# Selective scan: the products with C taken for two directions at once, u for four rows at once, and part of the diagonals on GpSimd

## The chip, the cores and the metric

The kernel runs on one core of a Trainium2 chip. A core has five engines that work side by side, each through its own list of instructions in order: TensorE (PE, with a separate record PEld for its weight loads), VectorE (DVE), ScalarE (ACT), GpSimd (POOL) and SyncE (SP), which here only issues DMA transfers. They meet through semaphores. SBUF is the working memory, PSUM the memory that PE writes; both have 128 partitions. The metric is the device time of one execution in microseconds (us).

## The reference, cut to what matters

Four images of 56 x 56 places and 128 channels go through four layers, each added to its input after a group normalization: attention (L0), a selective scan (L1), a deformable convolution (L2), attention again (L3). All is float32. Of L1, the scan is:

```python
delta = softplus(delta + delta_bias)               # 256 inner channels d, 3136 places
def step(h, inp):                                  # h: [4 directions of an image, d, 16 states n]
    u_i, d_i, b_i, c_i = inp
    dA = jnp.exp(d_i[..., None] * A)
    h = h * dA + (d_i * u_i)[..., None] * b_i[:, None, :]
    y = jnp.einsum('gdn,gn->gd', h, c_i)
    return (h, y)
# xs: the places row by row, column by column, and both reversed;
# delta, B and C are the same for the four directions
```

The four directions' y are brought back to the order of places and added. Of L2, nine offsets for each place say where four neighbours are to be read; the reading positions are the offsets plus a fixed table of places (tap and place, no data in it).

## The kernel before, in words

`run` takes the images one after the other, and in each the layers one after the other. The scan is `mamba_scan` (line 875). Channels lie on partitions, in two halves j of 128. The image's 56 rows are taken two at a time (a step s, 28 of them); a group g = 2s + j is such a step for one half, 56 groups an image. A unit u is one row r (of two) in one direction d (of four) of a group: 8 units a group, 448 an image. A chunk is two steps, 224 places, the piece in which delta, B and C come from DRAM (`chunk`, tiles `xd` and `dl`).

For each group, `inputs_of` (L982) makes: `du`, delta times u, for each direction on POOL (`mult`, L994), 112 places each; `da`, the 16 decays exp(delta A) on ACT (L1002); and `du` split into parts (`high` on ACT, `low` on POOL, `low2` on ACT), turned on PE and kept as `ut`. For each step, `rows` (L936) makes from B the diagonals `dgb` (`b_diag`, L952): B, turned on PE into the PSUM tile `pb`, times a mask of ones on the diagonal, [112, 16 x 28], two for each row, on DVE, 16 to 6 units ahead of the step's first unit; and from C the tile `cb`, C spread over all partitions.

A unit is then: `inputs` (L1048) multiplies `ut` with `dgb` on PE, which spreads du times B over 16 states x 56 places into a PSUM bank `dbu` (two such); `inject` (L1059, ACT) puts the carried state in front; `scan` (L1066, DVE) is one instruction over 16 x 58 columns into one half of the SBUF tile `hs`, which holds a pair of directions (three such tiles); `save` (L1070, ACT) keeps the last state; `weigh` (L1075, POOL) multiplies the 16 x 56 states with `cb`, in place; `add_up` (L1084, PE) adds the 16 states by transposing them into one PSUM tile `yt`; `sum_out` (L1093, ACT) copies a pair's sums to `ys`; and for a group `back` (L1100, PE) and `back_add` (L1105, DVE) add them to the result `ya`.

The order is written out by hand: nothing reorders it. The loop at L1116 goes through the units, and each engine's list is what the loop emits for it, with two dictionaries of further work by unit: `soon` (the decays) and `plan` (all else, by `at(t, f)`). In step u of the loop stand save(u-1), inputs(u+1), the decays, weigh(u-1), scan(u), inject(u+1), add_up(u-3), sum_out, and then `plan`. The tiles `pbt`, `pcb`, `pt` and `pyb` share two PSUM banks (tag `mm`).

In `deform` (L1232) the normalized image is written to a table in DRAM by eight DMAs on SP (L1279, table `tab`, filled with zeros once at the start of the program), the offsets are convolved on PE, the positions are made of the offsets plus `base`, the table of places, on DVE (L1315 to L1324), and POOL then issues nine indirect DMAs for each 112 places (L1248). `base` is one of the columns of the constants' pack, which is loaded into SBUF at the start and stays there.

Of the kernel before, what the change touches and what calls it, by code (L numbers as in the profile page):

```python
# [19 lines left out]
P = 128  # L20
HW = 56
# [33 lines left out]
def _swin_cols():  # L55
# [6 lines left out]
    "C": [("ident", 128), ("gmat", 128), ("center1", 128), ("center2", 128), ("others2", 128), ("ones1", 1), ("ones2", 1), ("lo", 1), ("dmask", TB), ("halves", HW), ("base", 2 * KK * NTB)],  # L62
# [16 lines left out]
class _Net:  # L79
    def __init__(self, ctx, tc, x, packs, out):  # L80
# [5 lines left out]
        self.w = {}  # L86
        for i, (layer, cols) in enumerate(COLS.items()):
            at, n = _offsets(cols)
            t = wp.tile([P, n], F32, tag=f"w_{layer}", name=f"w_{layer}")
            (nc.sync if i % 2 == 0 else nc.scalar).dma_start(t, packs[layer])  # L90
            self.w[layer] = {name: t[:, o : o + k] for name, (o, k) in at.items()}
# [783 lines left out]
    def mamba_scan(self, b, xa, ya, s1):  # L875
# [10 lines left out]
        with tc.tile_pool(name="ms", bufs=2) as sb, tc.tile_pool(name="ms_ps", bufs=2, space=PSUM) as ps, tc.manual_schedule():  # L886
# [12 lines left out]
            def chunk(c):  # L899
# [31 lines left out]
                at(first - 22, high)  # L931
                at(first - 20, low)
                at(first - 18, low2)
                at(first - 14, both)

            def rows(s):  # L936
# [13 lines left out]
                def b_diag(r, tb):  # L950
                    t = m[r, tb] = sb.tile([TK, NST, TB], F32R, tag="dgb", name="dgb", bufs=8)
                    nc.vector.tensor_tensor(  # L952
                        t,
                        m["pb"][:TK, tb * NX + DTR : tb * NX + DTR + NST][:, :, None].to_broadcast([TK, NST, TB]),
                        dmask[:, None, :].to_broadcast([TK, NST, TB]),
                        ALU.mult,
                    )
# [15 lines left out]
                for r in range(2):  # L973
                    t = first - 16 + 8 * r
                    at(t, lambda r=r: b_rows(r))
                    for tb in range(2):
                        at(t + 1 + tb, lambda r=r, tb=tb: b_diag(r, tb))
# [4 lines left out]
            def inputs_of(g):  # L982

# [7 lines left out]
                def mult(d):  # L991
                    if d == 0:
                        m["du"] = sb.tile([P, 4, 2 * HW], F32, tag="du", name="du", bufs=1)
                    nc.gpsimd.tensor_tensor(m["du"][:, d, :].rearrange("p (r t) -> p r t", t=HW), dl(), self.direction(xa[:, j, :], d, 2 * s, 2), ALU.mult)  # L994
# [9 lines left out]
                def high():  # L1004
                    m["dh"] = sb.tile([P, 4, 4, 4, TB], F32R, tag="dh", name="dh", bufs=1)
                    du = m["du"].rearrange("p d (s t) -> p (d s) t", t=TB)
                    nc.scalar.copy(flat(m["dh"])[:, :, 0:2, :], du[:, :, None, :].to_broadcast([P, 16, 2, TB]))

                def low():
                    du = m["du"].rearrange("p d (s t) -> p (d s) t", t=TB)  # L1010
                    nc.gpsimd.tensor_tensor(flat(m["dh"])[:, :, 2, :], du, flat(m["dh"])[:, :, 0, :].bitcast(F32), ALU.subtract)
# [9 lines left out]
                def keep(i):  # L1021
                    m["ut", i] = sb.tile([TK, 4, P], F32R, tag="ut", name="ut", bufs=7)
                    nc.scalar.copy(m["ut", i].rearrange("k d c -> k (d c)"), m.pop(("pt", i))[:TK, :])

                for d in range(4):
                    at(first + d, lambda d=d: mult(d))
# [14 lines left out]
            def inputs(u):  # L1041
# [4 lines left out]
                for tb in range(2):  # L1046
                    for h in range(2):
# [3 lines left out]
                            rhs=made["r", g // 2][r, tb][:, 8 * h : 8 * h + 8, :].rearrange("k n t -> k (n t)"),  # L1051
# [9 lines left out]
            def scan(u):  # L1061
                g, r, d = units[u]
                if d % 2 == 0:
                    pairs[u // 2] = sb.tile([P, 2, NST, RW], F32, tag="hs", name="hs", bufs=3)
# [7 lines left out]
            def weigh(u):  # L1072
                g, r, d = units[u]
                hs = pairs[u // 2][:, d % 2, :, 2:]
                nc.gpsimd.tensor_tensor(hs, hs, made["r", g // 2]["cb"][:, :, r * HW : (r + 1) * HW], ALU.mult)  # L1075
# [15 lines left out]
            def sum_out(q):  # L1091
                backs[q] = sb.tile([YR, 2, P], F32, tag="ys", name="ys", bufs=6)
# [14 lines left out]
            for s in range(HW // 2):  # L1107
# [3 lines left out]
                for g in (2 * s, 2 * s + 1):  # L1111
                    inputs_of(g)
                    at(8 * g + 14, lambda g=g: back(g))
# [386 lines left out]
```

## Time and profile before

| what | value |
|---|---|
| median of 12 runs | 13417.06 us (13411.72 to 13436.87) |
| the profiled execution | 13425.0 us, its span 13423.2 us |
| busy over the span | PE 11694.9 us (87%), DVE 9588.2 (71%), ACT 7557.2 (56%), POOL 9942.3 (74%) |
| the scan of the first image, first scan to last | 995.19 to 2013.32 us |
| from the last scan to the first gather | 2013.32 to 2120.35 us |
| scans (L1066) | 1792, median 2068 ns |
| products with C (L1075) | 1792, median 1942 ns |

The profile is one execution. A group of instructions has a line of kernel.py, an engine, an operation, the tiles (out<-in) with shapes, a count, and then its busy time in us, the mean of one in ns, and the idle time of the engine just before them with what ended it. In the order of time a line has its start, its length, the instructions merged in it (x5) and, in brackets, the idle time before it. The 40 slices show the busy share of an engine in tenths; four images are four times ten slices. An instruction's record is somewhat longer than the distance to the start of the next one behind it, as they overlap a little.

### The profile page before, as it was taken

How to read it: one execution, taken by the hardware profiler on the slowest of the kernel's cores; microseconds unless marked ns; L12 is line 12 of the kernel's file. 1: busy time of each engine (PE TensorE's matmuls, PEld its weight loads, DVE VectorE, ACT ScalarE, POOL GpSimd, SP SyncE). 2: the span in 40 equal slices, each digit the busy share in tenths (PEclk: the TensorE clock that was granted, in tenths of full speed). 3: DMA queues.
4: the chain of work that ended last, by engine and by line, in shares of the span. 5: the costliest groups of instructions: out<-in, count | busy, mean ns of one | idle time of the engine just before them, and what ended most of it. 6: DMA issues, size and time to landing. Idle time of an engine off the chain costs nothing. (4 is left out here: it accounts for less than half of the span.)

```text
span 13423.2 us, 218271 instructions
## 1 busy us (share of the span) xinstructions
PE 11694.9 (87%) x85716; PEld 7453.1 (56%) x85716; DVE 9588.2 (71%) x11883; ACT 7557.2 (56%) x19130; POOL 9942.3 (74%) x6852
## 2 busy tenths in 40 slices
PE   8989994699998999469999899946999989994699
PEld 4448883444544888344454488834445448883444
DVE  6659995664664999656466599955646659995664
ACT  5567762356556776235655677623565567762356
POOL 4949994397594999439759499943975949994397
PEclk9999996799998999679999999967999999996799
DMA  1000004200000000420000000041000000004100
GB/s 57 1 13 5 4 4 121 62 1 9 2 1 13 5 4 4 123 60 1 10 2 1 13 5 4 4 128 55 1 10 2 1 13 5 4 4 129 54 1 6
DMA packets 155651, 317.99 MB, mean 24 GB/s; under 512 B 19660, under 2 KB 89344, under 8 KB 154496
## 3 DMA queue, kind: packets, MB, share of 16 engines
q0 software_dynamic: 80640, 231.28, 6.1%
q1 hardware_dynamic: 73696, 71.21, 1.7%
q8 instruction: 678, 11.11, 0.4%
q14 instruction: 349, 2.86, 0.1%
q10 hardware_dynamic: 288, 1.53, 0.0%
HBM read 256.04 MB, written 47.90 MB: 23 GB/s over the span
## 5 line engine op out<-in xcount | busy, mean ns | idle before, releaser
L555 POOL TENSOR_TENSOR es<-es,e 128x896 f32<-128x896 f32 x2016 | 4158.8, 2088 | 134.2 <-ACT e L549 76.0
L350 DVE TENSOR_REDUCE mx<-pm 128x1 f32<-128x512 f32 (+1 forms) x4928 | 3058.4, 671 | 1408.6 <-PE pm L349 793.1
L549 ACT ACTIVATE e<-pst 128x448 f32<-128x448 f32 (+1 forms) x5600 | 2677.8, 544 | 1895.8 <-PE pst L547 1349.1
L1066 DVE TENSOR_TENSOR_SCAN hs<-da,dbu 128x928 f32<-128x928 f32 x1792 | 3632.7, 2070 | 53.4 <-ACT dbu L1059 30.9
L1075 POOL TENSOR_TENSOR hs<-hs,cb 128x896 f32<-128x896 f32 x1792 | 3471.5, 1949 | 26.1 <-ACT carry L1070 20.6
L349 PE MATMUL pm<-ks,qs 32*128 32x512 f32 (+1 forms) x9856 | 2914.1, 636 | 13.4 <-DVE nm L371 7.8
L547 PE MATMUL pst<-qs,ks 32*128 32x448 f32 x11200 | 2687.1, 548 | 0.0
L1084 PE MATMUL yt<-w_C,hs 128*116 128x128 f32 x14336 | 1865.3, 273 | 1.2 <-POOL hs L1075 1.2
L542 PE MATMUL pst<-nm,sel 32*128 32x448 f32 x5600 | 1639.4, 615 | 0.0
L1084 PEld LDWEIGHTS yt<-w_C,hs 128*116 128x116 f32 x14336 | 1570.4, 135 | 2.1 <-POOL hs L1075 2.1
L1048 PE MATMUL dbu<-dgb,ut 112*128 112x224 f32 x7168 | 1258.4, 298 | 269.0 <-DVE hs L1066 268.8
L1248 POOL DMA_INDIRECT g<-tab,idx x1008 | 940.9, 933 | 563.0 <-issue 286.5
L571 PE MATMUL po<-e,va 128*32 128x448 f32 (+1 forms) x11200 | 1353.1, 551 | 0.1
L349 PEld LDWEIGHTS pm<-ks,qs 32*128 32x128 f32 x9856 | 924.3, 186 | 746.3 <-DVE mx L350 620.2
L1048 PEld LDWEIGHTS dbu<-dgb,ut 112*128 112x128 f32 x7168 | 945.3, 192 | 534.5 <-DVE hs L1066 524.5
L1362 PE MATMUL pvt<-w_C,g 112*128 112x112 f32 x2016 | 401.9, 364 | 920.2 <-issue 705.1
L1002 ACT ACTIVATE da<-dl,A 128x112 f32<-128x112 f32 x3584 | 1194.4, 382 | 0.1
L547 PEld LDWEIGHTS pst<-qs,ks 32*128 32x128 f32 x11200 | 1098.7, 185 | 102.2 <-issue 13.7
L542 PEld LDWEIGHTS pst<-nm,sel 32*128 32x128 f32 x5600 | 570.7, 184 | 741.1 <-DVE mx L350 387.8
L1363 ACT COPY vt<-pvt 128x336 f32<-128x336 f32 x336 | 142.0, 440 | 1365.4 <-remote 728.3
L1362 PEld LDWEIGHTS pvt<-w_C,g 112*128 112x128 f32 x2016 | 318.5, 202 | 1009.5 <-issue 761.0
L1070 ACT COPY carry<-hs 128x32 f32<-128x32 f32 x1792 | 397.5, 222 | 623.6 <-DVE hs L1066 615.6
(230 smaller groups left out, 15751.2 us busy)
## 6 DMA issues: line engine op xcount, KB each, us to landing
g<-tab,idx POOLq DMA_INDIRECT x1008
tab<-zero SPq DMA_DIRECT2D x4, 3364.0 KB
dl_d<-dl SPq DMA_DIRECT2D x28, 448.0 KB
dl<-dl_d SPq DMA_DIRECT2D x56, 224.0 KB
tab<-gt SPq DMA_DIRECT2D x16, 448.0 KB
out_dram<-x SPq DMA_DIRECT2D x28, 224.0 KB
tab<-gt SPq DMA_DIRECT2D x16, 336.0 KB
x<-in_x_dram SPq DMA_DIRECT2D x21, 224.0 KB
```

Source lines behind the costliest of these rows:

```text
L349: nc.tensor.matmul(pm[:, :m], lhsT=qs[head(h), q.start : q.start + P], rhs=ks[head(h), keys], start=True, stop=True)
L350: nc.vector.tensor_reduce(mx[:, home[i][1], h, kc : kc + 1], pm[:, :m], AX.X, ALU.max)
L542: nc.tensor.matmul(t[:, :CH], lhsT=self.sel[head(h), :], rhs=nm[head(h), part(qc)], start=True, stop=False)
L547: nc.tensor.matmul(t[:, :CH], lhsT=ks[head(h), k * KB : (k + 1) * KB], rhs=qs[head(h), part(qc)], start=False, stop=True)
L549: nc.scalar.activation(e[:nk, j, :], t[:nk, :CH], AF.Exp, scale=SCALE)
L555: nc.gpsimd.tensor_tensor(s, es[g - 1, p][:nk] if k == 1 else s, e[:nk], ALU.add)
L571: nc.tensor.matmul(m["po"][head(h), :CH], lhsT=va[:nk, k, head(h)], rhs=src(h)[:nk], start=(k == 0), stop=(k == NKB - 1))
L1002: nc.scalar.activation(m["da"][:, :, n, 2:], dl(), AF.Exp, scale=A[:, j, n : n + 1])
L1048: nc.tensor.matmul(pu[:, 8 * h : 8 * h + 8, 2 + tb * TB : 2 + (tb + 1) * TB], lhsT=made[g]["ut", 2 * r + tb][:, d, :], rhs=made["r", g // ...
L1066: nc.vector.tensor_tensor_scan(flat(pairs[u // 2][:, d % 2]), flat(made[g]["da"][:, r]), flat(banks.pop(u)), 0.0, ALU.mult, ALU.add)
L1075: nc.gpsimd.tensor_tensor(hs, hs, made["r", g // 2]["cb"][:, :, r * HW : (r + 1) * HW], ALU.mult)
L1084: nc.tensor.matmul(sums[q][:YR, e * P : (e + 1) * P], lhsT=hs[:, n, :], rhs=self.ident, start=(n == 0), stop=(n == NST // 2 - 1), is_trans ...
```

## The change

Products with C: `weigh` takes a pair of directions in one POOL instruction of 2 x 16 x 56 columns, in every second step of the loop, after the second of the two scans. `hs` has four buffers in place of three. `add_up` stands two steps later, `sum_out`, `back` and `back_add` two steps later too.

u: `mult` takes the four rows of a chunk in one instruction of 224 places for each half and direction, three units apart, for the first step of the chunk from nine units earlier to one unit later than before; its tile `du` stays for both steps of the chunk. ACT's copy `high` is two instructions in place of one.

Diagonals: `b_diag` makes both 28-place blocks of a row in one instruction of 2 x 16 x 28 columns. For two of each five rows it stands on POOL; ACT first copies B out of PSUM for these (`b_copy`). All stand some eight units later than before. Three tiles of double size in place of eight.

The chunk's splitting of B and C (`high`, `low`, `low2`, `both`) stands up to six units later. `ut` has six buffers (seven), `ys` five (six).

Room in SBUF: `base` leaves the constants' pack and is loaded by DMA on SP in each image's `deform`, after the stores of the table; the zeros' tile is half as wide, and the fill of the tables goes in pieces of 128 columns. The weights' packs L0 to L3 change places between the two issuing queues, as the position in the list decides.

```diff
-    "C": [..., ("halves", HW), ("base", 2 * KK * NTB)],
+    "C": [..., ("halves", HW)],
+    "P": [("base", 2 * KK * NTB)],
...
+            if layer == "P":
+                continue
...
-                at(first - 22, high)
-                at(first - 20, low)
-                at(first - 18, low2)
-                at(first - 14, both)
+                at(first - 16, high)
+                at(first - 15, low)
+                at(first - 13, low2)
+                at(first - 12, both)
...
-                def b_diag(r, tb):
-                    t = m[r, tb] = sb.tile([TK, NST, TB], F32R, tag="dgb", name="dgb", bufs=8)
-                    nc.vector.tensor_tensor(
-                        t,
-                        m["pb"][:TK, tb * NX + DTR : tb * NX + DTR + NST][:, :, None].to_broadcast([TK, NST, TB]),
-                        dmask[:, None, :].to_broadcast([TK, NST, TB]),
-                        ALU.mult,
+                mine = lambda r: (2 * s + r) % 5 in (1, 3)
+
+                def b_copy(r):
+                    if mine(r):
+                        pb = m["pb"]
+                        m["pb"] = sb.tile([TK, 2 * NX], F32, tag="pbc", name="pbc", bufs=1)
+                        nc.scalar.copy(m["pb"], pb[:TK, : 2 * NX])
+
+                def b_diag(r):
+                    t = m[r] = sb.tile([TK, 2, NST, TB], F32R, tag="dgb", name="dgb", bufs=3)
+                    b = m["pb"][:TK, : 2 * NX].rearrange("k (b n) -> k b n", b=2)[:, :, DTR : DTR + NST, None]
+                    (nc.gpsimd if mine(r) else nc.vector).tensor_tensor(
+                        t, b.to_broadcast([TK, 2, NST, TB]), dmask[:, None, None, :].to_broadcast([TK, 2, NST, TB]), ALU.mult
                     )
...
                     t = first - 16 + 8 * r
+                    t += 7
                     at(t, lambda r=r: b_rows(r))
-                    for tb in range(2):
-                        at(t + 1 + tb, lambda r=r, tb=tb: b_diag(r, tb))
+                    at(t + 1, lambda r=r: b_copy(r))
+                    at(t + 2 if mine(r) else t + 1, lambda r=r: b_diag(r))
...
-                        m["du"] = sb.tile([P, 4, 2 * HW], F32, tag="du", name="du", bufs=1)
-                    nc.gpsimd.tensor_tensor(m["du"][:, d, :].rearrange("p (r t) -> p r t", t=HW), dl(), self.direction(xa[:, j, :], d, 2 * s, 2), ALU.mult)
+                        src["du", j] = sb.tile([P, 4, SC], F32, tag=f"du{j}", name="du", bufs=1)
+                    rows = lambda t: t.rearrange("p (r t) -> p r t", t=HW)
+                    nc.gpsimd.tensor_tensor(rows(src["du", j][:, d, :]), rows(src["dl"][:, j, :]), self.direction(xa[:, j, :], d, 2 * s, 4), ALU.mult)
...
-                    nc.scalar.copy(flat(m["dh"])[:, :, 0:2, :], du[:, :, None, :].to_broadcast([P, 16, 2, TB]))
+                    for k in range(2):
+                        nc.scalar.copy(m["dh"][:, :, :, k, :], du())
...
                 for d in range(4):
-                    at(first + d, lambda d=d: mult(d))
+                    if s % 2 == 0:
+                        at(first - 9 + 4 * j + 3 * d, lambda d=d: mult(d))
...
-            def weigh(u):
-                g, r, d = units[u]
-                hs = pairs[u // 2][:, d % 2, :, 2:]
-                nc.gpsimd.tensor_tensor(hs, hs, made["r", g // 2]["cb"][:, :, r * HW : (r + 1) * HW], ALU.mult)
+            def weigh(q):
+                g, r, d = units[2 * q]
+                hs = pairs[q][:, :, :, 2:]
+                cb = made["r", g // 2]["cb"][:, None, :, r * HW : (r + 1) * HW]
+                nc.gpsimd.tensor_tensor(hs, hs, cb.to_broadcast([P, 2, NST, HW]), ALU.mult)
...
-                    at(8 * g + 14, lambda g=g: back(g))
+                    at(8 * g + 16, lambda g=g: back(g))
                     for d in range(4):
-                        at(8 * g + 15 + d // 2, lambda g=g, d=d: back_add(g, d))
+                        at(8 * g + 17 + d // 2, lambda g=g, d=d: back_add(g, d))
...
-                if 0 <= u - 1 < nu:
-                    weigh(u - 1)
+                if u % 2 == 0 and 0 <= u - 2 < nu:
+                    weigh((u - 2) // 2)
...
-                if 0 <= u - 3 < nu:
-                    add_up(u - 3)
-                if 0 <= u - 4 < nu and u % 2 == 1:
-                    sum_out((u - 5) // 2)
+                if 0 <= u - 5 < nu:
+                    add_up(u - 5)
+                if 0 <= u - 7 < nu and u % 2 == 1:
+                    sum_out((u - 7) // 2)
...
-        z = self.keep.tile([116, 2 * P], F32, tag="z", name="zero")
+        z = self.keep.tile([116, P], F32, tag="z", name="zero")
...
-                base = self.w["C"]["base"][:QB, :]
+                base = sb.tile([QB, 2 * n2], F32, tag="base", name="base")
+                nc.sync.dma_start(base, self.places[:QB])
```

## The prediction

> **What bounds the kernel now.** I read the busy shares and the 40 slices first: four equal images, and in each a stretch of some 1,018 us in which VectorE (DVE) and GpSimd (POOL) are both at nine tenths or more. That is the scan, the only stage with large edits. Next the stage windows, for the shares inside it:
>
> ```profile
> DVE  6659995664664999656466599955646659995664
> POOL 4949994397594999439759499943975949994397
> ...
> 995.19:2013.32 1018.13, 943.71 (x7649) 851.90 (x7649) 1008.20 (x773) 730.84 (x2509) 1011.84 (x785) 0.99 0.02 4
> ```
>
> Columns of the last line: stage, its length, then busy us of PE, PEld, DVE, ACT, POOL, then clock and DMA. DVE 99%, POOL 99%: the shares alone do not say which sets the pace. The costliest groups of 1100 to 1900 us name the work:
>
> ```profile
> L1066 DVE TENSOR_TENSOR_SCAN hs<-da,dbu 128x928 f32<-128x928 f32 x351 | 712.0, 2069 | 4.7
> L1075 POOL TENSOR_TENSOR hs<-hs,cb 128x896 f32<-128x896 f32 x352 | 679.4, 1940 | 1.1 <-ACT carry L1070 0.8
> L994 POOL TENSOR_TENSOR du<-dl,xa 128x112 f32<-128x112 f32 x175 | 79.5, 454 | 0.0
> L1105 DVE TENSOR_TENSOR ya<-ya,pyb 128x112 f32<-128x112 f32 x176 | 54.6, 310 | 3.0
> L952 DVE TENSOR_TENSOR dgb<-pbt,w_C 112x448 fp32r<-112x448 f32 x88 | 52.6, 598 | 0.0
> L1011 POOL TENSOR_TENSOR dh<-du,dh 128x448 fp32r<-128x448 f32 x44 | 50.1, 1138 | 0.0
> ```
>
> Queued instructions overlap a little, so I cost by the distance from one start to the next, which the order of time gives:
>
> ```profile
> 1509.72 0.60 DVE L952 TENSOR_TENSOR dgb<-pbt,w_C 112x448 fp32r<-112x448 f32 x1
> 1510.24 2.08 DVE L1066 TENSOR_TENSOR_SCAN hs<-da,dbu 128x928 f32<-128x928 f32 x1
> ...
> 1512.75 9.99 DVE L1066 TENSOR_TENSOR_SCAN hs<-da,dbu 128x928 f32<-128x928 f32 x5
> 1522.65 0.66 DVE L1105 TENSOR_TENSOR ya<-ya,pyb 128x112 f32<-128x112 f32 x2
> 1527.98 0.59 DVE L952 TENSOR_TENSOR dgb<-pbt,w_C 112x448 fp32r<-112x448 f32 x1
> ```
>
> ```profile
> 1501.29 0.15 POOL L998 MEMSET da<- 128x64 f32 x1
> 1501.40 3.83 POOL L1075 TENSOR_TENSOR hs<-hs,cb 128x896 f32<-128x896 f32 x2
> 1505.19 1.13 POOL L1011 TENSOR_TENSOR dh<-du,dh 128x448 fp32r<-128x448 f32 x1
> 1506.29 3.83 POOL L1075 TENSOR_TENSOR hs<-hs,cb 128x896 f32<-128x896 f32 x2
> 1510.09 0.42 POOL L994 TENSOR_TENSOR du<-dl,xa 128x112 f32<-128x112 f32 x1
> 1519.38 0.17 POOL L998 MEMSET da<- 128x64 f32 x1
> ```
>
> Five scans take 1522.65 - 1512.75 = 9.90 us. One period (8 scans, half a 2-row step) is 18.26 us from diagonal to diagonal, and it repeats to 0.01 us. Averaged over 1100 to 1900 us, DVE's period is 8 scans x 1.987 + 4 sums x 0.289 + 0.175 idle before those + 2 diagonals x 0.516 = **18.255**: it is filled, so DVE sets it. POOL's is 8 products x 1.897 + 4 du x 0.417 + low part 1.096 + memset 0.104 + a quarter of the chunk's 0.62 = **18.20**, only 0.05 behind.
>
> **The change, part by part.** All sums are against the profiled execution's 13425.0 us (span 13423.2 plus 1.8 around it); the median of 12 is 7.9 below it.
>
> *Diagonals, DVE.* One instruction of 896 columns takes the place of two of 448. A DVE product of 896 elsewhere (L1189) has 1.075 us against 0.598 for 448, so the second half adds 0.477: 0.516 + 0.477 = 0.99 from start to start. Three of five stay on DVE: per period 1.031 goes, 0.6 x 0.99 = 0.59 comes, and DVE needs **17.82**, 0.44 less.
>
> *Products with C, POOL.* Four of 1792 for eight of 896. The trace has no 1792; what merging saves is one fixed part. Bounds: nothing saved (pair 3.795), or the 448-row's line (1.897 against 1.096 puts 0.296 in the fixed part, pair 3.50). A slower rate per element, as L555's 2.088 for 896 has, would be an excess: 2 x 2.088 = 4.18 less a fixed part of 0.19 is 3.99, the dear end. I take the line through the same access form, L1075 and L994: 1.897 - 0.417 over 784 elements is 1.89 ns each, fixed 0.205; with the unstrided du alone (0.38) it is 0.165. Pair 3.61: 0.185 saved, 0.74 a period.
>
> *u for four rows, POOL.* Eight instructions of 224 a chunk for sixteen of 112: two fixed parts a period, 0.37. They now lead by up to nine steps more; dl is loaded eight steps before, against the 3 us that this load takes (979.3 to 982.3).
>
> *Diagonals on POOL.* 0.4 a period of 896 elements. Nearest row by size L1075, 1.90; by access (one operand repeated along the inner dimension) L275, 784 in 1.498, which gives 1.68 with 0.205 of it fixed; dear end L555, 2.05. I take 1.90: 0.76. So POOL needs 18.20 - 0.74 - 0.37 + 0.76 = **17.83**. The Trainium skill, GPSIMD Engine Reference, section Engine selection, speaks against this part: two-input elementwise work belongs on VectorE, GpSimd being about twice as slow. The rows agree on the factor (0.99 against 1.90); by the rule the change adds work, 0.36 us a period, or +80 us over all, if engine time counted; by the rows what counts is the fuller of two engines.
>
> *Waits that the new order adds.* A diagonal for r = 1 on POOL is issued two steps before PE wants it, behind a product pair; PE's later inputs and transposes queue behind that wait, then ACT's carry copy, then the scan. From the end of scan 16s-1: 0.3 + 3.6 + 1.9 = 5.8 against PE's 3 x 1.99 + 0.66 = 6.6, and some 1.6 more before DVE notices: POOL may run 2.4 us late. Low part and a du just before make it 0.7 to 1.4 late. Elsewhere: the last du of the second half is written one step before ACT's copy of it; in two of twenty periods POOL is late enough there to hold ACT, and with it the carry copy, by 0.8 us: 0.08 a period. The bank for `back` may be freed only by DVE's diagonal: 0.1 x 0.6. I book 0.13 on DVE's 17.82, hence **17.95** a period; below zero nothing (it is a delay), the upper end is in rival 3. What is late next is POOL, at 17.83.
>
> *Steady sum.* 4 images x 55 periods x (18.255 - 17.95) = **-67.1 us**.
>
> *Head of the scan, +3.4 an image.* Before, the chunk's low part ran on POOL at 981.17, before dl had landed; now three du of 0.63 stand ahead of it, so it ends at 984.85, ACT's low2 and two copies at 986.0, the exponential's table load (1.28) at 987.3 against 984.2, and ACT is filled from there to the first scan. Ends: 0 if only du's own 0.8 counts elsewhere, 5.
>
> *Tail, +2.2.* The last scan ended at 2013.33 and the next stage began at 2020.6. The last product now holds both directions (+1.7) and two transposes follow it instead of one (+1.0); some of it runs beside `back`. Ends 1 and 4.
>
> *base by DMA, +3.8.* The table of places left SBUF; each image now loads 112 x 504 floats on SP, queued behind the eight stores of the table, which SP issues until 2115.8:
>
> ```profile
> 2102.73 13.06 SPq L1279 DMA_DIRECT2D tab<-gt  x8
> 2112.13 0.46 DVE L1315 TENSOR_TENSOR pos<-pof,w_C 112x288 f32<-112x288 f32 x1 [9.49 <-PE pof L1308]
> 2120.35 1.13 POOL L1248 DMA_INDIRECT g<-tab,idx  x1 [23.81 <-DMA tab<-gt]
> ```
>
> The addition at L1315 ran at 2112.13 and idx was ready 3.1 later, five before the gather that waited for the stores. The load is as large as dl's (224 KB, 3.0 us): alone it lands at 2118.8, behind the stores' last bytes at 2121.0. Then idx is ready at 2124.1, 3.8 after the gather began, and 252 gathers of 1.24 us back to back move with it. Ends 1.6 and 5.
>
> Head, tail and base: 4 x 9.4 = **+37.6**.
>
> *The rest at nothing.* The start: the C pack is 252 KB smaller; at the some 400 GB/s of the start x lands 0.6 earlier, **-0.6**; L0 to L3 change queues, and only x is waited for last. The zero fill in pieces of 512 bytes: it ended near 160 us and the first store to it is at 2102; it could be ten times slower. ACT's extra copies (0.29 for the split of `high`, 0.4 x 0.25 for the copy out of PSUM) lie beside an ACT that is 72% busy; were it full, 0.39 a period, 86 us. Fewer ut, dgb and ys: each is free three or more steps before its next use.
>
> Sum: 13425.0 - 67.1 + 37.6 - 0.6 = 13394.9; less 7.9 for the median, **13387**.
>
> **Rivals.**
> 1. *GpSimd has room after all* (pair near 3.50, diagonals 1.68, no lateness): DVE's 17.82 stands, -220 x 0.435 = -96 + 37 = -59, 13358. For: L275 and the 448-row. Against: the fixed part in the same access form.
> 2. *The pair saves nothing:* POOL needs 18.20 - 0.37 + 0.76 = 18.59, so +74 + 37, 13528. Slower from a pair of 3.70 on (POOL 18.20). For: L555 shows that GpSimd's rate can differ by 7% between forms.
> 3. *POOL's diagonals come late*, the other side: 88 of them, each holding PE, ACT and the scan. From 0.67 us each the gain is used up ((96 - 37) / 88); at 1.2 us the time is 13358 + 106 = 13464. For: POOL is full and in order. Against: the 2.4 us of room above.
> 4. *PE takes over.* Its matmuls of a period, start to start, are some 16.9 of 18.2; with waits in order it may hold 18.1: -34 + 37, no change, 13420.
>
> **How the numbers follow.** Forecast 0.45, its own range 13360 to 13420; rival 1 0.20, rival 2 0.08, rival 3 0.17, rival 4 0.10. A change within 0.2% (27 us) is about what a measurement of this kernel cannot tell from none. Below 13390 lie 0.26 of the forecast and rival 1: 0.46; same is 0.19 + 0.10 + 0.03 of rival 3: 0.32; slower 0.14 + 0.08: 0.22. The range reaches from below rival 1 to the middle of rival 3, 13335 to 13455, and leaves out rival 2 and the dear half of 3.
>
> **What would show it.** A period of 17.95 between equal scans; 1792 products at 3.6 from start to start, POOL diagonals at 1.9, DVE's at 0.99; idle time before scans that ends with ACT's carry copy, under 0.2 a period; the first gather waiting for DVE and 4 us later after its stores; first scan 3 us later after dl lands. Wrong it is if products of 1792 stand above 3.7, if scans wait behind PE for POOL's diagonals, or if base lands before the stores.

## The result and the profile after

The changed kernel takes 13532.99 us (median of 7 runs, 13524.09 to 13562.64), the kernel before 13417.62 (28 runs): the ratio is 1.009, 95% interval 1.008 to 1.0099. It is **115 us slower** where 13387, 30 faster, was predicted. The profiled execution has a span of 13528.9 us for 13423.2, +105.7.

Where that lies, summed over the four images, from the same points in both traces (mean of an image in brackets):

| stretch | predicted | measured |
|---|---|---|
| first chunk's first step to first scan | +13.6 (3.4) | +12.8 (14.48 to 17.68) |
| first scan to last scan | -67.1 | **+88.8** (1018.39 to 1040.59) |
| last scan to first gather | +24 (2.2 and 3.8) | +18.7 (105.65 to 110.31) |
| all else | -0.6 | -14.6 |

"All else" (the gathers and the other layers) was not taken apart; in the run of the kernel before with `base` alone loaded anew (below, on another chip) the same stretches came out 19 us shorter, so from this record 14.6 can't be told from what executions differ by. So the ends came out about as said, and the miss is in the scan. Its first image after, by the stage windows (stage, length, then busy us of PE, PEld, DVE, ACT, POOL, then clock and DMA):

```profile
998.70:2035.50 1036.80, 952.98 (x7649) 887.98 (x7649) 989.82 (x699) 725.05 (x2583) 1000.34 (x471) 0.96 0.02 4
```

DVE's busy time fell from 1008 to 990 and POOL's from 1012 to 1000, as the change wants; the stage is 19 us longer all the same. No engine fills it any more: POOL is at 96%, DVE at 95%. What was gained in work was lost, and more, in waiting. The costliest groups of 1100 to 1900 us, DVE and POOL:

```profile
L1083 DVE TENSOR_TENSOR_SCAN hs<-da,dbu 128x928 f32<-128x928 f32 x343 | 691.6, 2068 | 20.8 <-ACT dbu L1076 17.0
L1124 DVE TENSOR_TENSOR ya<-ya,pyb 128x112 f32<-128x112 f32 x172 | 55.0, 320 | 19.8 <-PE pyb L1119 14.7
L966 DVE TENSOR_TENSOR dgb<-pbt,w_C 112x896 fp32r<-112x896 f32 x26 | 27.7, 1064 | 0.0
L1094 POOL TENSOR_TENSOR hs<-hs,cb 128x1792 f32<-128x1792 f32 x173 | 641.9, 3718 | 26.5 <-ACT carry L1087 26.5
L1008 POOL TENSOR_TENSOR du<-dl,xa 128x224 f32<-128x224 f32 x86 | 63.7, 741 | 0.0
L966 POOL TENSOR_TENSOR dgb<-pbc,w_C 112x896 fp32r<-112x896 f32 x17 | 29.9, 1757 | 0.0
```

Look at the last column. DVE now idles 20.8 us ahead of scans and 19.8 ahead of sums, where it idled 4.7 and 3.0; POOL idles too, until ACT's `save` (L1087), so at those moments it waits for the scan as the scan waits for others. And the prices of the instructions are right: start to start, a pair product takes 3.66 (predicted 3.61), a du 0.68 (0.63), a diagonal on POOL 1.70 (1.90) and on DVE 0.98 (0.99). (The mean lengths in the table are longer, as records overlap.) POOL's work is 4 x 3.66 + 2 x 0.68 + 1.10 + 0.11 + 0.16 + 0.4 x 1.70 = 18.05 us a period, DVE's 17.8; both are less than the 18.255 of before. Yet the mean period is 18.66: (1040.59 - 14.4) / 55, where 14.4 is what the stage of before has beyond 55 x 18.255. Single periods of the stretch from 1100 to 1900 us, from first scan to first scan, go from 17.15 to 21.46, where those of before lie between 18.25 and 18.27.

Who is waited for? The waits of the same stretch (us in total, times, longest). Left out are rows that the kernel before has too, of ACT and PE for the scan and of `inject` for PE, and PE's own rows beside those of its weight loads; the last line is the one row of these that the list of before has:

```profile
PEld pcb L976 <- ACT cb L982: 28.2, 43, 2.1
PEld pyb L1119 <- DVE dgb L966: 21.8, 21, 1.2
DVE hs L1083 <- ACT dbu L1076: 17.0, 18, 2.5
ACT dh L1024 <- POOL du L1008: 16.5, 10, 2.3
DVE ya L1124 <- PE pyb L1119: 14.7, 8, 2.7
PEld dbu L1065 <- POOL dgb L966: 4.9, 6, 1.0
...
PEld pcb L965 <- ACT cb L971: 16.8, 44, 0.4
```

The scan waits for ACT (`inject`), ACT for POOL's u, PE for ACT's copy `cb`. A late diagonal on POOL, the cause that the prediction weighed as a rival, holds PE for only 4.9 us, 6 times. How one leads to the other is seen in the order of time at the start of a chunk (rows that don't bear on it are left out):

```profile
1499.75 1.76 POOL L966 TENSOR_TENSOR dgb<-pbc,w_C 112x896 fp32r<-112x896 f32 x1
1500.17 10.00 DVE L1083 TENSOR_TENSOR_SCAN hs<-da,dbu 128x928 f32<-128x928 f32 x5
1501.45 3.72 POOL L1094 TENSOR_TENSOR hs<-hs,cb 128x1792 f32<-128x1792 f32 x1
1505.12 0.67 POOL L1008 TENSOR_TENSOR du<-dl,xa 128x224 f32<-128x224 f32 x1
1505.73 3.72 POOL L1094 TENSOR_TENSOR hs<-hs,cb 128x1792 f32<-128x1792 f32 x1
1509.40 0.80 POOL L1008 TENSOR_TENSOR du<-dl,xa 128x224 f32<-128x224 f32 x1
1510.23 1.03 ACT L1024 CAST dh<-du 128x448 fp32r<-128x448 f32 x2 [2.29 <-POOL du L1008]
1511.86 0.18 ACT L1076 COPY dbu<-carry 128x32 f32<-128x32 f32 x1
1512.13 2.09 DVE L1083 TENSOR_TENSOR_SCAN hs<-da,dbu 128x928 f32<-128x928 f32 x1 [1.96 <-ACT dbu L1076]
1512.24 0.52 ACT L982 COPY cb<-pcb 128x448 f32<-128x448 f32 x1
1512.81 0.66 PE L976 MATMUL pcb<-x,ident 104*128 104x112 f32 x4 [1.98 <-ACT cb L982]
...
1515.89 2.32 PE L1119 MATMUL pyb<-w_C,ys 116*128 116x56 f32 x16
1518.24 0.69 DVE L1124 TENSOR_TENSOR ya<-ya,pyb 128x112 f32<-128x112 f32 x2 [1.05 <-PE pyb L1119]
```

The last u of a chunk's second half stands on POOL behind a diagonal and two pair products and ends at 1510.20. ACT has waited 2.29 us for it, to copy it into `dh`; nothing needs that copy at once, but behind it in ACT's list stands the carry copy of the next unit (`inject`, L1076), and DVE stands still for 1.96 us. Behind that stands the copy out of `cb`'s bank, for which PE waits 1.98 us, and behind PE's wait stands `back`, so that DVE waits again, 1.05 us, for the sums.

The wait of PE alone would not do that. Shortly behind it the trace shows PE's granted clock halved, while the multiplications and transposes ahead of `back`, and its first ones, run (the clock is the third number from the end):

```profile
1513.40:1516.70 3.30, 3.30 (x18) 3.30 (x17) 3.30 (x3) 1.38 (x6) 3.30 (x3) 0.50 0.00 0
```

Taken over the 52 places where a chunk follows another: at 37 the clock was halved within 6 us of the chunk's first scan, and DVE then idled 1.1 to 2.7 us ahead of the sums of the second unit; at the other 15 it idled 0.33 at most, and at seven of these PE had waited 1.3 to 1.9 us all the same. `back`'s matmuls stand 0.213 us apart under the halved clock and 0.112 under the full one. Over the first image's scan the mean clock is 0.96, where it was 0.99 before.

Over all four images, the waits around the tile `du`, before and after:

```profile
its engine sat idle before it (us, times) until:
  ACT dh L1007: 29.8, 8
  DMA dl<-dl_d: 2.1, 4
...
  POOL du L1008: 76.6, 45
  ACT dh L1024: 30.8, 8
  DMA dl<-dl_d: 11.9, 4
```

The kernel before has no row of POOL there; now 45 of the 52 places where a chunk follows another show it. Added up by the unit of the scan, DVE idles 58.7 us before the first unit of a chunk, and 71.9 us before the sums in its second unit.

### The profile page after: what moved, and what is told of

Same layout as the page of the kernel before. It is cut to its first block, busy times and chain, and to the rows that moved or that the text cites. A ratio compares the mean times of both kernels' runs of the same rounds, so it can differ in the third digit from the quotient of the medians.

```text
span 13528.9 us, 217603 instructions
## 1 busy us (share of the span) xinstructions
PE 11742.4 (87%) x85716; PEld 7609.9 (56%) x85716; DVE 9513.8 (70%) x11571; ACT 7538.7 (56%) x19442; POOL 9909.5 (73%) x5596
## 5 line engine op out<-in xcount | busy, mean ns | idle before, releaser
L1094 POOL TENSOR_TENSOR hs<-hs,cb 128x1792 f32<-128x1792 f32 x896 | 3317.8, 3708 | 159.8 <-ACT carry L1087 158.6
L1103 PE MATMUL yt<-w_C,hs 128*116 128x128 f32 x14336 | 1946.8, 281 | 29.8 <-POOL hs L1094 28.6
L1103 PEld LDWEIGHTS yt<-w_C,hs 128*116 128x116 f32 x14336 | 1635.1, 139 | 47.9 <-POOL hs L1094 44.0
L1065 PE MATMUL dbu<-dgb,ut 112*128 112x224 f32 x7168 | 1295.8, 305 | 110.0 <-DVE hs L1083 89.8
L1065 PEld LDWEIGHTS dbu<-dgb,ut 112*128 112x128 f32 x7168 | 987.3, 199 | 265.6 <-DVE hs L1083 199.8
L1076 ACT COPY dbu<-carry 128x32 f32<-128x32 f32 x1792 | 334.8, 187 | 790.0 <-PE dbu L1065 785.1
```

The source lines that it names most:

```text
L1065: nc.tensor.matmul(pu[:, 8 * h : 8 * h + 8, 2 + tb * TB : 2 + (tb + 1) * TB], lhsT=made[g]["ut", 2 * r + tb][:, d, :], rhs=made["r", g // ...
L1094: nc.gpsimd.tensor_tensor(hs, hs, cb.to_broadcast([P, 2, NST, HW]), ALU.mult)
L1103: nc.tensor.matmul(sums[q][:YR, e * P : (e + 1) * P], lhsT=hs[:, n, :], rhs=self.ident, start=(n == 0), stop=(n == NST // 2 - 1), is_trans ...
```

## The experiments

The runs went to several chips. On two of them (one for the runs with u one unit earlier, one later, three of ten, and the ends; another for `back` alone) the deformable convolution's gathers take 312 us an image, on the others 350 to 353. The kernel before is faster there too (13192 us on both, 13415 and 13409 on the others); so each run is compared with the kernel before on its own chip, and the length of the scan stage (mean of four images) stands beside it. In the scan stage a diagonal of 896 columns on DVE has 0.982 us from start to start in every run that has it, and a pair product 3.65 to 3.67, so stages are compared across chips too. Where no diff is said to start elsewhere, it starts from the changed kernel.

**u of the second half two units earlier**

```diff
-                        at(first - 9 + 4 * j + 3 * d, lambda d=d: mult(d))
+                        at(first - 9 + 2 * j + 3 * d, lambda d=d: mult(d))
```

> The changed kernel with the u of the second half written two units earlier. Theory T (the last of these four products stands one unit before ACT's copy of it and holds ACT, and behind it the copies that free the PSUM banks, PE and the scan): in the changed kernel the idle time of VectorE in the first three units of a chunk is 59 us before scans and 72 us before the sums over the four images, some 130 in all; it goes, the time falls from 13533 to about 13400, and the wait of ACT's copy on this product (77 us, 45 times) is gone. Rival R1 (GpSimd's diagonals come late for PE) and rival R2 (the bank of the return transposes is freed only by VectorE's diagonal): nothing of theirs moves, 13520 to 13540.

13398.77 us, ratio 0.999 (0.9981 to 0.9999); scan stage 1010.7. One number takes 134 us away, as theory T said. The waits around `du` are now

```profile
its engine sat idle before it (us, times) until:
  ACT dh L1024: 30.8, 8
  DMA dl<-dl_d: 11.7, 4
```

with POOL's line gone, and POOL, at 18.02 us of work a period, idles only 3.2 us of 800:

```profile
L1094 POOL TENSOR_TENSOR hs<-hs,cb 128x1792 f32<-128x1792 f32 x178 | 659.9, 3714 | 3.2 <-ACT carry L1087 3.1
```

So the late u is what made the change a loss, directly and by what follows from it. Without it the kernel is about as fast as before, and POOL is the bound.

**All diagonals on DVE**

```diff
-                mine = lambda r: (2 * s + r) % 5 in (1, 3)
+                mine = lambda r: False
```

> The changed kernel with all diagonals on VectorE. T: VectorE's period without idle is 18.255 - 1.031 + 0.982 = 18.21; GpSimd is 1.7 us less late twice in five periods, but the copy still waits for the product of one unit before at each of the 13 later chunks: 1.0 before the scan and 1.0 before the sums each, 4 x 13 x 2.0 = 104, so 13417 - 10 + 104 + 20 = about 13530, as the changed kernel. R1: the lateness goes with the diagonals, 13430. R2: more periods have VectorE's diagonal (all in place of three of five), the same or up to 20 us slower than the changed kernel.

13486.58 us, ratio 1.0052 (1.0037 to 1.0067); scan stage 1031.6. All three expectations missed: T's and R2's were too slow, R1's too fast. ACT's wait for u vanished here too: without diagonals POOL has 17.4 us of work a period and keeps up, so it takes both, u placed so close and a POOL that is behind, to make u late. But DVE with all ten of ten has 18.2, and another wait became regular (us, times, longest, in 800 us, 43 periods):

```profile
PEld pyb L1119 <- DVE dgb L966: 50.0, 43, 1.2
```

PE's `back` waits in every period for DVE's diagonal, whose turned B lies in the shared bank that `back` takes next. The change put both into the same step of the loop, `back` two units later than before and the diagonals on DVE six to seven later: 8g + 16 and 16s - 8 + 8r are both multiples of eight. This wait is taken up again below.

**u for two rows, as before the change**

```diff
-                        src["du", j] = sb.tile([P, 4, SC], F32, tag=f"du{j}", name="du", bufs=1)
+                        m["du"] = sb.tile([P, 4, 2 * HW], F32, tag="du", name="du", bufs=1)
...
-                    if s % 2 == 0:
-                        at(first - 9 + 4 * j + 3 * d, lambda d=d: mult(d))
+                    at(first + d, lambda d=d: mult(d))
```

> The changed kernel with u made for two rows at a time where the kernel before makes it. T: no copy of ACT waits for u; GpSimd's period grows from 18.05 by 4 x 0.417 - 2 x 0.679 = 0.31 to 18.36 and sets the pace: 220 x (18.36 - 18.255) = 23 over the kernel before, and 20 for the table of places and the ends: 13460. R1: GpSimd is fuller and its diagonals later: 13550 or more. R2: 13530.

13589.14 us, ratio 1.0121 (1.0106 to 1.0137), 130 more than T said and in the range that R1 gave; scan stage 1061.8, a period of 19.04 where POOL has 18.33 of work. R1's cause isn't what the trace shows: PE waits for POOL's diagonals 4.2 us of 800, 8 times. Four du of 112 places a period in place of two of 224 make POOL the fullest engine by far, and ACT waits for u twice as often:

```profile
its engine sat idle before it (us, times) until:
  POOL du L1007: 139.0, 88
```

The old placing of u does not heal the change. Before, it was early enough; whether that was for a POOL less behind or for its shorter products with C, between which u stood, this run doesn't separate.

**The kernel before, with `base` loaded by DMA and the packs as in the change**

```diff
...
-                base = self.w["C"]["base"][:QB, :]
+                base = sb.tile([QB, 2 * n2], F32, tag="base", name="base")
+                nc.sync.dma_start(base, self.places[:QB])
...
```

> The kernel before with the table of places loaded by DMA in each image (and the smaller pack of constants, the other order of the weights' loads), nothing else of the change. The prediction's term: +3.8 us an image between the last scan and the first gather, so 13417 + 15 - 1 = 13431. Rival: the load lands before the stores of the table and is hidden, 13417 (at most +1.6 an image, 13423).

13419.3 us, ratio 1.0004 (0.9995 to 1.0013), which can't be told from none. The first gather is 1.2, 0.7, 3.4 and 2.2 us later in the four images, 1.9 in the mean where 3.8 was predicted. In the changed kernel the order of time shows the load behind the eight stores, and the first gather waiting no longer for them but for DVE:

```profile
2123.26 12.71 SPq L1298 DMA_DIRECT2D tab<-gt  x8
2136.02 1.46 SPq L1310 DMA_DIRECT2D base<-in_P_dram  x1
2140.37 0.46 DVE L1335 TENSOR_TENSOR pos<-pof,base 112x288 f32<-112x288 f32 x1 [17.20 <-DMA base<-in_P_dram]
...
2143.75 1.13 POOL L1267 DMA_INDIRECT g<-tab,idx  x1 [26.31 <-DVE idx L1344]
```

The load is issued at 2136.02 and used at 2140.37: 4.3 us after its issue, not 5.2 as the prediction had it (stores until 2115.8, last bytes at 2121.0).

**u one unit earlier, and one unit later**

```diff
-                        at(first - 9 + 4 * j + 3 * d, lambda d=d: mult(d))
+                        at(first - 9 + 3 * j + 3 * d, lambda d=d: mult(d))     # one earlier
+                        at(first - 9 + 5 * j + 3 * d, lambda d=d: mult(d))     # one later
```

> The changed kernel with u of the second half written one unit earlier (the run before this: two). Theory T2 (GpSimd is late by its diagonals, and a product of u placed one unit before ACT's copy hands that lateness on to ACT and all behind it): the waits were 0.9 to 2.5 us before the scan, 1.3 on average; one unit is 2.0 us, so most of them go: 13400 to 13440, between the two. Rival R5 (the order of GpSimd's list matters, not the distance): no smooth step, 13533 or 13399.

> The changed kernel with u of the second half written one unit later, in the copy's own unit. T2: every one of the 52 later chunk ends waits up to 2.0 us more, before the scan and in part before the sums: +60 to +130, 13590 to 13660. R5: no step, 13520 to 13550.

One earlier: 13310.6 us, ratio 1.0093 (1.0078 to 1.0109), scan stage 1043.4, the same as the changed kernel; so lateness is not a matter of units, as R5 said. One later: 13539.2, ratio 1.0263 (1.0247 to 1.0279), scan stage 1099.4, some 230 us over the changed kernel where T2 had 130 at most and R5 nearly nothing. The waits around `du` of these two, the earlier one first:

```profile
  POOL du L1008: 66.7, 48
```

```profile
  POOL du L1008: 266.6, 52
```

The loop emits a pair product on POOL only in its even steps, ahead of what `plan` has for the step. The last u of the second half stands three units before the chunk, between the pair products of units -4 and -2. Four units before, it still stands between the same two; two units before, it falls behind the next one; five units before, it goes ahead of one, which is the 134 us of the first run. The place in the list counts, in steps of 3.66 us, and the number in `at` only where it moves u past a pair product.

**Three of ten diagonals on GpSimd, with u two units earlier**

```diff
-                mine = lambda r: (2 * s + r) % 5 in (1, 3)
+                mine = lambda r: (2 * s + r) % 10 in (2, 6, 8)
```

> The first run of this study (u of the second half two units earlier) with three of ten diagonals on GpSimd, all of a step's first row, in place of four. With the distances measured, GpSimd's period is 4 x 3.655 + 2 x 0.683 + 1.096 + 0.109 + 0.155 + 0.3 x 1.693 = 17.85 (it was 18.02, the period's mean length being 18.05), VectorE's 17.22 + 0.7 x 0.982 = 17.91. T2 with GpSimd as the bound: the period falls to some 17.95 to 18.0, -11 to -22, 13377 to 13388. Rival (waits for the bank of the return transposes or PE set 18.05): 13399.

13187.75 us, ratio 0.9996 (0.9987 to 1.0005), scan stage 1013.7, no better than two of five: T2's gain did not come. With POOL's work down to 17.85 and DVE's at 17.9, neither engine explains a period of 18.17.

**The ends, on top of that**

```diff
-                at(first - 16, high)
-                at(first - 15, low)
-                at(first - 13, low2)
-                at(first - 12, both)
+                k = 10 if c == 0 else 0
+                at(first - 16 - k, high)
+                at(first - 15 - k, low)
+                at(first - 13 - k, low2)
+                at(first - 12 - k, both)
...
+                base = sb.tile([QB, 2 * n2], F32, tag="base", name="base")
+                nc.sync.dma_start(base, self.places[:QB])
# the same two lines leave their place behind the stores of the table
```

> The same with the two ends mended: the table of places loaded ahead of the stores (its load alone cost 1.9 us an image), and the first chunk's split ahead of the products of u (the first scan starts 3.2 us later after the load than before the change): -4 x (1.9 + 3.2) = -20 against the run beside it, 13357 to 13368. Rival: both ends are hidden by what comes next (the first group's copies on ACT, the stores), no more than -5.

13159.86 us, ratio 0.9976 (0.9967 to 0.9985): 28 us less, where 20 were expected. The first scan comes 15.0 us after the chunk's first step (17.7 in the changed kernel, 14.5 before), the first gather 107.5 after the last scan (110.3, 105.65), and its wait is the stores' again:

```profile
2091.81 0.34 SPq L1284 DMA_DIRECT2D base<-in_P_dram  x1
...
2117.41 1.13 POOL L1268 DMA_INDIRECT g<-tab,idx  x1 [22.65 <-DMA tab<-gt]
```

**`back` and its sums one unit later**, on top of that; the ends with two of five diagonals; and both

```diff
-                    at(8 * g + 16, lambda g=g: back(g))
+                    at(8 * g + 17, lambda g=g: back(g))
                     for d in range(4):
-                        at(8 * g + 17 + d // 2, lambda g=g, d=d: back_add(g, d))
+                        at(8 * g + 18 + d // 2, lambda g=g, d=d: back_add(g, d))
```

> The kernel with six of twenty diagonals on GpSimd and the ends mended, with one more edit: `back` and the sums behind it one unit later each. In that kernel PE's `back` waits 33 us of 800 for DVE's diagonal to free its bank (31 times), and DVE stands idle 38 us ahead of scans and 31 ahead of sums over the four scan stages. If that wait is on the path (B), the waits for the diagonal go and 20 to 30 us of DVE's idle time with them: scan stages of some 1007 us for 1012.9, a ratio to the kernel before of 0.9955 to 0.996 for 0.9976. If PE has room enough that the wait costs nothing (N), the waits go and the time stays: scan stages 1012 to 1014, ratio 0.997 to 0.998.

> The changed kernel with u of the second half two units earlier, two of five diagonals on GpSimd as the change has them, and the ends mended (base's load ahead of the table's stores, the first chunk's own steps ten units earlier). Scan stages were 1010.7 us with two of five and 1013.7 with three of ten; if the parts add up (A), this is 10 to 14 us under the kernel with three of ten and both ends mended: ratio 0.9966 to 0.997, scan stages 1010. If at two of five GpSimd, which is full, takes the gain at the ends back (F), it stands at 0.9976 or above, with scan stages of 1013 or more.

> The kernel with two of five diagonals on GpSimd and the ends mended, and `back` and its sums one unit later. There GpSimd, at 18.02 us a period, is the fuller engine, and `back` waits for DVE's diagonal 25 us of 800. If the fuller engine sets the period whatever PE waits for (A, N), this is within 5 us of the kernel without the edit; if the wait is on the path (B), it gains 15 us or more on it.

| kernel (all with u earlier and the ends) | us | ratio (interval) | scan stage | period |
|---|---|---|---|---|
| three of ten, `back` as changed (other chip) | 13159.86 | 0.9976 (0.9967 to 0.9985) | 1012.9 | 18.15 |
| three of ten, `back` later | **13313.92** | **0.9927 (0.9913 to 0.994)** | 997.2 | 17.87 |
| two of five, `back` as changed | 13372.77 | 0.9971 (0.996 to 0.9982) | 1010.3 | 18.11 |
| two of five, `back` later | 13348.33 | 0.9953 (0.994 to 0.9967) | 1005.5 | 18.02 |

With `back` one unit later at three of ten the kernel is 95 us faster than before, and the stage lost 15.7 us where 6 were expected of the edit. The wait at the bank was on the path, and cost more than DVE's idle time shows: that falls from 17 to 10 us an image, but the scans also come queued again, so that they stand 1.989 us from start to start in place of 1.995 (448 of them, 2.4 us), and the sums 0.268 in place of 0.297 (224, 6.5 us). 7 + 2.4 + 6.5 is about the whole 15.7; these are its parts, not a cause. PE's clock was halved 47 times in the four scan stages without the edit and 2 times with it; how much of the gain is the wait's and how much the clock's, no run separates. In the order of time a period is now two runs of scans with two pairs of sums between them, and PE's wait has moved to where it holds neither DVE nor POOL for long:

```profile
1513.83 1.06 DVE L967 TENSOR_TENSOR dgb<-pbt,w_C 112x896 fp32r<-112x896 f32 x1
...
1514.82 4.05 DVE L1084 TENSOR_TENSOR_SCAN hs<-da,dbu 128x928 f32<-128x928 f32 x2
...
1515.39 1.89 PE L1120 MATMUL pyb<-w_C,ys 116*128 116x56 f32 x16
...
1518.79 0.67 DVE L1125 TENSOR_TENSOR ya<-ya,pyb 128x112 f32<-128x112 f32 x2
...
1521.92 9.98 DVE L1084 TENSOR_TENSOR_SCAN hs<-da,dbu 128x928 f32<-128x928 f32 x5
1522.12 0.88 POOL L1009 TENSOR_TENSOR du<-dl,xa 128x224 f32<-128x224 f32 x1
1522.15 0.62 PE L1036 MATMUL pt<-w_C,dh 128*112 128x128 f32 x4 [1.64 <-DVE ya L1125]
```

The groups of 1100 to 1900 us show little idle time on DVE and none on POOL:

```profile
L1084 DVE TENSOR_TENSOR_SCAN hs<-da,dbu 128x928 f32<-128x928 f32 x358 | 721.9, 2067 | 4.3 <-ACT dbu L1077 3.3 <-POOL da L1016 0.6
L1125 DVE TENSOR_TENSOR ya<-ya,pyb 128x112 f32<-128x112 f32 x180 | 55.7, 310 | 5.0 <-PE pyb L1120 1.8
L1095 POOL TENSOR_TENSOR hs<-hs,cb 128x1792 f32<-128x1792 f32 x180 | 677.8, 3793 | 0.0
```

At two of five the edit brings 24 us, as B said, and the period is then POOL's 18.02. (The ends with two of five, without the edit, came out nearly as A said, 0.9971.) POOL idles 0.1 us of 800 there, and 0.0 at three of ten, where its work is 17.85 for a period of 17.87; DVE's scans, sums and diagonals are 17.67 from start to start, and 0.21 idle. So in both POOL is the bound once the waits are gone, with DVE close behind at three of ten.

**`back` one unit later alone**, u and diagonals as in the changed kernel (the diff is the last one)

> The changed kernel with one edit: `back` and its sums one unit later; u and the diagonals stay as the change has them. If ACT's wait for the late u is the cause of the loss (U), it is still there at some 44 of 52 chunk ends, and only the wait for the bank of `back` goes, worth what it was worth at two of five diagonals with u earlier (4.8 us an image) or up to double: 20 to 40 us, ratio 1.006 to 1.0075. If the late u does its harm by way of `back` (the idle time ahead of the sums, 95 us over four stages, most of it in the first steps of a chunk), the step's room takes most of it away (K): 70 us or more, ratio 1.0035 or less.

13232.15 us, ratio 1.0031 (1.0019 to 1.0043), scan stage 1023.9; the changed kernel has 1.009, and 1.0093 with u one unit earlier on the other chip on which the kernel before takes 13192 us, so about 78 us are gone. The size is that of the second expectation, but what the first one said of ACT holds too: it waits for u at all 52 places,

```profile
  POOL du L1008: 98.7, 52
```

and DVE idles 80.6 us ahead of the first unit of a chunk, but 41.5 ahead of sums where it was 94.7. PE's clock is still halved at 36 of the 52 places, but `back`'s matmuls, a unit later, mostly stand behind the halved stretch. So the late u does its harm in two ways, at once by the carry copy, and by way of PE's clock and `back`, and the room of one unit takes away most of the second. The two fixes overlap: 134 us for u alone, about 78 for `back` alone, and `back` brings 24 when u is already early.

## Why the prediction was wrong

**What failed** is "Waits that the new order adds". It named the right place, "the last du of the second half is written one step before ACT's copy of it", and booked it as late "in two of twenty periods" by 0.8 us, 0.08 a period. It was late at 45 of 52 chunk ends, one period in five, and the run that moves it shows its whole cost: 1040.6 - 1010.7 = 29.9 us a stage, 0.54 a period, seven times the term. The 0.71 between the forecast's 17.95 and the 18.66 measured are, to 0.01, this 0.54, 0.09 for the bank of `back` and 0.07 by which POOL's own work (18.02 with u earlier) lies above 17.95. Three things went into the 0.54:

- Its room was taken from steps of the loop and not from POOL's list. The pair product ahead of it can't begin before its second scan is done. In the stretch shown that scan ends at 1502.2 and ACT comes to the copy at 1507.94; the pair product and u take 3.66 + 0.68, so 1.4 us are left with POOL on time. One diagonal ahead (1.70), or a low part and a du (1.78), uses that up, and here POOL began that pair product 3.5 us after the scan, at 1505.73. The runs that move u or POOL's work agree: late with less room (one unit later) or with a fuller POOL (u for two rows), not late with 4 us more room or with no diagonals on POOL.
- What stands behind the waiting instruction was counted on ACT alone (the carry copy). PE's wait for `cb`'s bank, the halved clock behind it and `back` under that, and so the second wait of DVE, were not followed; the sum has PE at one speed throughout.
- DVE and POOL wait for each other by turns: DVE for u, and then POOL, 26.5 us of 800, for ACT's carry copy after the scans. The sum had only the fuller engine's work and waits on DVE.

**Also mis-sized: "The bank for `back` may be freed only by DVE's diagonal: 0.1 x 0.6".** It is one step of the loop for both, so PE waited in 21 of 43 periods (26 had their diagonal on DVE), about 1 us each. Removing it brought 4.8 us a stage (0.09 a period) at two of five, where POOL's work left no more to gain, but 15.7 (0.29) at three of ten.

**And mis-sized: POOL's 17.83.** The prediction's own terms, 18.20 - 0.74 - 0.37 + 0.76, add up to 17.85, and 18.05 was measured: the pair product was 0.05 dearer (0.2 a period) and the du 0.05 (0.1), the diagonals 0.2 cheaper (0.08). That alone is above the forecast's period, so at two of five 17.95 was not to be had with all waits gone; the kernels without them stand at 18.02 there, and at 17.87 at three of ten.

**What was right.** DVE's work after, 17.8 a period for 17.82, and that both engines were full before. That "what is late next is POOL" holds. The head (3.2 an image for 3.4) was right; tail and `base` together came to 4.7 for 6.0, `base` alone to 1.9 for 3.8, since the load came in closer behind the stores than booked. GpSimd takes 1.70 us for a diagonal and DVE 0.98, a factor of 1.7 where the Trainium skill (GPSIMD Engine Reference, Engine selection) has about two. Its advice to keep such work on VectorE is not borne out by the runs as such: three of ten on GpSimd is the fastest kernel, and all on DVE, with u late no more, is at 1.0052; no run has all diagonals on DVE with `back` moved as well.

**The rivals.** The third, "POOL's diagonals come late", is nearest: POOL's lateness, held in line on another engine until the scan waits. But it came by u and ACT; PE waited for POOL's diagonals 4.9 us of 800. The first (DVE's 17.82 stands) failed on POOL's 18.05, and the second (a pair saves nothing) on 3.66 for the pair, under its point of 3.70 though only just. The fourth (PE holds 18.1) is not borne out, as with both waits moved a period is 17.87; but PE had a part that it didn't name, by its clock.

## What to carry to other kernels

Joining short instructions on an in-order engine saves their fixed parts (0.13 us a pair of products, 0.15 a pair of du here), but it makes the list coarse: a short instruction between two long ones can move only by a whole long one, so its slack must be reckoned from its place in the list, not from the step that it is written in. When producer and consumer are moved, write down, for each consumer that may come late, what stands behind it on its engine, and who waits for that, through every engine to the one that sets the pace; here it went u, ACT, carry copy, scan, and again ACT, `cb`'s bank, PE, its clock, `back`, sums. A wait of PE is to be read together with the granted clock behind it: without the halved clock a wait of 1.3 to 1.9 us cost DVE 0.33 us at most. And when two steps that share a PSUM bank are moved, look at whether they now fall into the same step; giving one of them a step of room took some 78 us off by itself. Together with u two units earlier, fewer diagonals on GpSimd and the earlier work at the ends it turned a change that was 115 us slower into one that is 95 us faster.

## What the runs showed of the hardware

A GpSimd product whose operand is repeated along the inner dimension took 1.70 us for 896 columns of 112 partitions, less than the strided product of 896 on 128 partitions of before (1.90). DVE's scans stand 1.987 us from start to start in the kernel before and 1.989 in the fastest one, and 1.992 to 2.001 in the kernels where they wait more often, with no idle time shown for the difference; sums the same, 0.268 to 0.297. PE's granted clock was halved 63 times in the four scan stages of the changed kernel, 97 us a stage, and 1 and 2 times in those of the kernel before and the fastest one, 12 and 10 us a stage. And the same 252 gathers of an image took 312 us on two chips and 350 to 353 on the others; the gathers of the kernel before were traced on one of the others only.
